# A layernorm's reciprocal deviation by Newton's steps on GpSimd, in a layernorm, attention and feed-forward kernel

## The chip, the cores and the metric

The kernel runs on one core of one Trainium2 chip. The metric is the device time of one execution in microseconds, as the median of several runs. Engines are named as the profile does: PE is TensorE, PEld its weight load, DVE is VectorE, ACT is ScalarE, POOL is GpSimd, SP is SyncE, which here only issues DMAs.

## The reference

Four sequences of 512 tokens and 512 features are normalized; the normalized tokens go through causal attention with 16 heads of 128 and, beside it, through a gated feed-forward network; the attention's output times silu of the network's is added to the input.

```python
def _layernorm(x, axis=-1, eps=1e-05):
    m = jnp.mean(x, axis=axis, keepdims=True)
    v = jnp.var(x, axis=axis, keepdims=True)
    return (x - m) / jnp.sqrt(v + eps)

x = L0_attn_x                              # (4, 512, 512)
xn = _layernorm(x, axis=-1)
s = _L0_attn_ref(xn, W_Q, W_K, W_V, W_O, b_Q, b_K, b_V, b_O)   # causal softmax attention
g = _silu(_L0_ffn_ref(xn, gate_w, up_w, down_w, gate_s, up_s, down_s))
x = x + s * g
```

Only the normalization changes. It is a small part of the work, but everything else of a batch starts from it.

## The kernel before

Tokens are worked in tiles of 128 on the partitions: a batch has four tiles (NT = 4), a row of features four chunks (ND = 4). Every operand of a matmul is kept as a high part and a low part (`Split`), and a product is made of three matmuls, so each result that TensorE leaves in PSUM is taken out twice: ScalarE writes the high part (L295, L321, L358, L516), then VectorE subtracts it from the PSUM value for the low part (L296, L323, L359, L517).

The order of work on each engine is the order of the program text (`manual_schedule`). Each engine works through its own queue in that order, and an instruction that waits holds up all behind it.

**Layernorm of a batch.** `ln_stats` makes mean and variance of each tile on VectorE (two instructions for each tile, L226 and L227). `ln_sd` takes the square root for all four tiles on ScalarE (L234), for which the activation table must be changed; `table` (L243) loads the exponential's table again with a dummy activation. `ln_scales` makes the reciprocal and the shift, minus mean times reciprocal, on VectorE (L255, L257), each 128x4. `ln_normalize` makes the normalized tile xn, on VectorE (L273) or, for some tiles, on ScalarE (L270). `ln_transposes` turns it on TensorE (L290) into a PSUM tile `tr`; ScalarE copies that to xh (L295) and VectorE subtracts to xl (L296, `ln_low`). Batch 0 is normalized tile by tile ahead of everything; batches 1, 2 and 3 are normalized among the attention heads.

**The loop over heads.** A step n is a head (g, b, i): head group g (eight, of two heads each), batch b, head i of the group. For group 0 these are heads 0 and 1 for batch 0, heads 2 and 3 for batch 1, and so on. In one step the program issues:

1. `softmax` of this head: score matmuls (L104, L394, L395) into PSUM tiles `sc`, masked maxima on VectorE (L403), exponentials on ScalarE (L417), reciprocals of the sums on VectorE (L420), and the scaling p times rtot on GpSimd (L423), each for row tiles of 512, 384, 256 and 128 columns. A list `between` is worked off between these.
2. `split_p` of the head before (for the first heads; later after step 3): probabilities that came back from DRAM transposed (`ptr`) are cast on ScalarE (L470) and subtracted on VectorE (L472, both inputs in SBUF; `pt`).
3. v projections of the first two tiles, then `turn_p`: VectorE transposes the scaled p in 32x32 blocks (L437) and a DMA writes them to DRAM and four DMAs read them back (`turn`, `ptr`).
4. `project`: q and k of the next head (L104, taken out in L358 and L359).
5. `attend` of the head before: z (L504, taken out in L516 and L517), then v projections of the other two tiles or the output projection (`pso`, L93 to L95, added up in L560 and L563).

Batch 1 is normalized in step 0, batch 2 in step 2, batch 3 in step 4 (`ln_next`); their statistics are made in steps 0 (and shortly ahead of it), 1 and 3. The transposes of the normalized tiles are mixed into the v projection's matmuls: a list `side` is popped once after each matmul, and begins with a few empty entries, so that the transposes start late enough. The v projection of a tile can also be begun early (`begin_v`, `finish_v`).

PSUM has eight banks: three for `st` (scores, and the `tr` tiles of batches 1 to 3 but the last of each) and five for `mm` (q, k, v, z, output projection, the last `tr`), taken in turn. A tile that has not been read out for its low part holds its bank, and TensorE waits for it. From group 1 on, `chores` do other work for the network on GpSimd (L608) and VectorE. The network follows the last head.

Of the kernel before, what the change touches and what calls it, by code (L numbers as in the profile page):

```python
# [10 lines left out]
F32 = mybir.dt.float32  # L11
# [7 lines left out]
P = 128  # L19
HG = 2  # L20
IGNORE = -100000.0
EPS = 1e-5
BIG = 3.0e38
WARM = 20
# [18 lines left out]
def kernel(  # L43
# [78 lines left out]
    with ExitStack() as at:  # L122
# [21 lines left out]

        here.tile([P, 8], F32, name="pad")
        ident = here.tile([P, P], F32, name="ident")
# [104 lines left out]
        def ln_scales(b):  # L251

            mv, sd = sd_of.pop(b)
            rstd = small.tile([P, NT], F32, name="rstd4", bufs=2)
            nc.vector.reciprocal(rstd, sd)  # L255
            add = small.tile([P, NT], F32, name="shift", bufs=2)
            nc.vector.scalar_tensor_tensor(add, mv[:, :, 0], -1.0, rstd, ALU.mult, ALU.mult)  # L257
            scaled[b] = rstd, add

        def ln_normalize(b, t, on_scalar=False):  # L260
            xt = x_in.pop((b, t))
            mv, sd = ln_of.pop((b, t))
            xn = lnp.tile([P, D], F32, name="xn")
            if b in scaled:
                rstd, add = (a[:, t : t + 1] for a in scaled[b])
            else:
                rstd = small.tile([P, 1], F32, name="rstd")
                nc.vector.reciprocal(rstd, sd)
            if on_scalar:
                nc.scalar.activation(xn, xt, AF.Identity, bias=add, scale=rstd)  # L270
                xn_of[b, t] = xn
                return
            nc.vector.tensor_scalar(xn, xt, mv[:, 0:1], rstd, ALU.subtract, ALU.mult)  # L273
            xn_of[b, t] = xn
# [101 lines left out]

        def softmax(qT, kT, between):
            p = pp.tile([P, NS * P], F32, name="p", tag="p")
# [34 lines left out]
            for pack in PACK:  # L413
                for t in pack:
                    tot = small.tile([P, 1], F32, name="tot", bufs=8)
                    rtot = small.tile([P, 1], F32, name="rtot", bufs=8)
                    nc.scalar.activation(  # L417
                        of[t], of[t], AF.Exp, bias=nmax[t], scale=-1.0, accum_out=tot
                    )
                    nc.vector.reciprocal(rtot, tot)  # L420
                    if len(between) > NT // 2:
                        between.pop(0)()
                    nc.gpsimd.tensor_scalar(of[t], of[t], rtot, 1.0, ALU.mult, ALU.mult)  # L423
# [213 lines left out]
        with tc.manual_schedule():  # L637
# [34 lines left out]
            for low, on in zip(wv_lows, (nc.gpsimd, nc.vector)):  # L672
                low(on)
            prepare_qk(1, -1)

            q_of = project(0, 0, wq[0], bq_sb, "q", 2, by_pass=True)
# [11 lines left out]
            ln_low(0, 2)  # L688
            ln_low(0, 3)
            table(AF.Exp)  # L690
            for _ in v_first:
                pass
            v_second = project_v_steps(0, 0, 1)
            next(v_second)
            for t in range(NT):
                load_x(1, t)
            for of in (q_of, k_of) * 3:
                next(of)
            qT = next(q_of)
            mv = ln_stats(1, range(NT), slice(0, 1))  # L700
            kT = next(k_of)
            split_pending(-1)
            ln_stats(1, range(NT), slice(1, 2), mv)
            for _ in v_second:
# [28 lines left out]
            for n, (g, b, i) in enumerate(heads):  # L733
# [26 lines left out]
                if ln_next:  # L760
                    norms = [lambda: ln_scales(b + 1)] + [
                        lambda t=t: ln_normalize(b + 1, t, t < NT // 2 if n > 0 else t == NT - 1)
                        for t in ((2, 3, 0, 1) if n > 0 else range(NT))
                    ]
                if ln_next and 0 not in begun and n > 0:

                    begin_v(g, b, 0)
                elif 0 in begun:
                    finish_v(0)
                of = softmax(qT, kT, norms if n > 0 else [])  # L770
                if n > 0 and early:
# [6 lines left out]
                if n == 0:  # L778
                    ln_stats(ln_b, range(NT), slice(2, NT), mv)
                if nxt is not None:  # L780
# [4 lines left out]
                if nxt is not None:  # L785
                    if ln_b is not None and n > 1:
                        ln_stats(ln_b, range(NT))
                    nh = nxt[0] * HG + nxt[2]
                    if n == 0:
                        ln_sd(ln_b, range(NT))  # L790
                        table(AF.Exp)
                        while norms:
                            norms.pop(0)()
                    *_, qT = project(nxt[1], nh, wq[nh], bq_sb, "q")
# [24 lines left out]
                if g > 0:  # L819
                    next(chore)  # L820
                if n == 2:

                    begin_v(g, b, half)
                if before is not None:
                    attend_last(before, pt)
                if n == 1:
                    ln_stats(ln_b, range(NT))
                if n == 1:

                    begin_v(nxt[0], nxt[1], 0)  # L830
                    next(begun[0])
                if ln_b is not None and n > 0:
                    ln_sd(ln_b, range(NT))
                    table(AF.Exp)
                if ln_next:
                    side.extend([lambda: None] * (2 * ND + (NT - 1 if n == 0 else 0)))
                    for t in range(NT):
# [589 lines left out]
```

## Time and profile before

| | us |
|---|---|
| median of 3 runs | 1196.64 (1196.04 to 1197.71) |
| the profiled execution, its own time | 1196.86 |
| its span, from the first to the last instruction | 1195.1 |

| engine | busy us | share of the span |
|---|---|---|
| PE | 1184.2 | 99% |
| DVE | 921.7 | 77% |
| ACT | 608.2 | 51% |
| POOL | 453.9 | 38% |

The granted TensorE clock is 0.999 of full speed over the span. A line of the timeline gives start, duration, engine, line, operation, output and inputs, shape, and how many instructions it merges; in brackets is the engine's idle time just before it and what ended it. A merged line has the shape of its first instruction. In the table of waits the numbers are total time, times and the longest. Matmuls are pipelined and their ends are modelled, so small gaps between them are best read from their starts.

### The profile page before, as it was taken

Reading aid. Unit: us, or ns where it says so; the run is one execution under the profiler, and the core shown is the slowest. Engines: PE = TensorE matmul, PEld = TensorE weight load, DVE = VectorE, ACT = ScalarE, POOL = GpSimd, SP = SyncE. Lnnn points to the kernel's source line nnn. Section 1 sums busy time; section 2 is a strip of 40 time slices with the busy share of each in tenths; the row PEclk is TensorE's granted clock in tenths of the full one; section 3 lists DMA queues with packets and bytes.
Section 4 is the critical chain, followed back from the end, with each engine's and each line's share of the span. In section 5 each row is a group of like instructions: output and inputs, shape, how many; then the busy total and the mean of one; then the engine's idle time right before and its main releaser. Section 6 shows DMA issues by size and latency. Waiting matters only on the chain.

```text
span 1195.1 us, 20226 instructions
## 1 busy us (share of the span) xinstructions
PE 1184.2 (99%) x6478; PEld 1036.2 (87%) x6478; DVE 921.7 (77%) x2485; ACT 608.2 (51%) x1455; POOL 453.9 (38%) x636
## 2 busy tenths in 40 slices
PE   9999999999999999999999999999999999999997
PEld 8888888888888888888888888888888888989896
DVE  7887777778777877787878777877777778959574
ACT  6764444545455545544554454545454454637372
POOL 4312342434253424342443344324232374636250
PEclk9999999999999999999999999999999999999999
DMA  5554456666675667566756676766565797969691
GB/s 167 156 181 152 148 165 208 203 194 211 194 218 179 203 202 223 172 214 205 225 183 205 199 229 175 216 185 197 164 183 156 215 328 233 265 203 267 179 264 56
DMA packets 131506, 236.75 MB, mean 198 GB/s; under 512 B 14912, under 2 KB 58688, under 8 KB 131392
## 3 DMA queue, kind: packets, MB, share of 16 engines
q1 hardware_dynamic: 73584, 133.86, 36.4%
q10 hardware_dynamic: 29520, 53.40, 15.4%
q0 software_dynamic: 28288, 48.12, 14.2%
q8 instruction: 54, 0.88, 0.3%
q14 instruction: 60, 0.49, 0.1%
HBM read 150.51 MB, written 84.80 MB: 197 GB/s over the span
## 4 chain that ended last, share of the span: by engine, by line
PE 98%; DVE 1%; DMA 0%; ACT 0%; issue 0%
PE psq L104 15%; PE psk L104 15%; PE psv L330 9%; PE z L504 9%; PE sc L104 8%; PE pd L1151 7%; PE px L981 6%; PE pso L93 5%; PE pso L94 5%; PE pso L95 5%; PE psv L334 4%; PE pz L981 3%; PE psv L104 2%; PE py L981 2%; PE pu L981 1%; PE pg L981 1%
## 5 line engine op out<-in xcount | busy, mean ns | idle before, releaser
L423 POOL TENSOR_SCALAR p<-p,rtot 128x512 f32<-128x512 f32 (+3 forms) x256 | 136.5, 554 | 434.2 <-DVE rtot L420 413.4
L417 ACT ACTIVATE p<-p,nmax 128x512 f32<-128x512 f32 (+3 forms) x256 | 140.9, 552 | 122.8 <-DVE nmax L403 122.7
L330 PE MATMUL psv<-wv,xh 128*128 128x512 f32 x448 | 124.6, 400 | 0.0
L437 DVE STREAM_TRANSPOSE sq<-p 128x256 f32<-128x256 f32 x378 | 113.3, 363 | 0.0
L104 PE MATMUL sc<-k,q 128*128 128x512 f32 (+2 forms) x576 | 112.1, 338 | 1.2 <-DVE xl L296 0.8
L104 PEld LDWEIGHTS sc<-k,q 128*128 128x128 f32 x576 | 98.9, 188 | 12.4 <-ACT xh L295 1.0
L358 ACT ACTIVATE k<-psk,consts 128x512 fp32r<-128x512 f32 (+1 forms) x65 | 44.4, 683 | 114.0 <-PE psk L104 114.0
L403 DVE CUSTOM_DVE_ANT_0 p<-sc,mask 128x512 f32<-128x512 f32 (+2 forms) x192 | 96.2, 550 | 0.6 <-PE sc L104 0.4
L470 ACT CAST pt<-ptr 128x640 fp32r<-128x640 f32 x126 | 85.2, 725 | 17.7 <-DMA ptr<-turn 10.7
L359 DVE SCALAR_TENSOR_TENSOR k<-psk,consts,k 128x512 fp32r<-128x512 f32 (+1 forms) x65 | 48.0, 739 | 58.5 <-ACT k L358 58.5
L472 POOL TENSOR_TENSOR pt<-ptr,pt 128x640 fp32r<-128x640 f32 x53 | 83.7, 1579 | 19.1 <-ACT pt L470 14.3
L330 PEld LDWEIGHTS psv<-wv,xh 128*128 128x128 f32 x448 | 76.0, 188 | 10.0
L334 PEld LDWEIGHTS psv<-wv,xl 128*128 128x128 f32 x448 | 68.4, 188 | 9.5
L420 DVE RECIPROCAL rtot<-tot 128x1 f32<-128x1 f32 x256 | 41.5, 162 | 41.2 <-ACT p L417 34.4
L563 DVE TENSOR_TENSOR a<-pso,a 128x512 f32<-128x512 f32 x108 | 69.6, 684 | 3.6 <-DMA a<-acc 3.2
L334 PE MATMUL psv<-wv,xl 128*128 128x256 f32 x448 | 71.0, 280 | 0.0
L1151 PE MATMUL pd<-wd,hl 128*128 128x512 f32 (+1 forms) x187 | 69.7, 378 | 0.0
L472 DVE TENSOR_TENSOR pt<-ptr,pt 128x640 fp32r<-128x640 f32 x73 | 67.8, 940 | 2.4 <-ACT pt L470 2.3
L1151 PE MATMUL pd<-wd,hh 128*128 128x512 f32 (+1 forms) x187 | 69.6, 377 | 0.0
L358 ACT ACTIVATE q<-psq,consts 128x512 fp32r<-128x512 f32 (+1 forms) x65 | 44.3, 681 | 42.1 <-PE psq L104 41.8
L970 POOL DMA_DIRECT2D ws<-sum x78 | 41.5, 540 | 37.5 <-PE px L981 34.3
L504 PE MATMUL z<-pt,v_0h 128*128 128x512 f32 x128 | 50.6, 396 | 0.1
(623 smaller groups left out, 3258.6 us busy)
## 6 DMA issues: line engine op xcount, KB each, us to landing
turn<-sq SPq DMA_DIRECT2D x63, 640.0 KB, 2.9
ptr<-turn SPq DMA_DIRECT2D x252, 160.0 KB, 5.4
acc<-a SPq DMA_DIRECT2D x124, 256.0 KB, 2.8
a<-acc ACTq DMA_DIRECT2D x108, 256.0 KB, 3.1
ws<-sum POOLq DMA_DIRECT2D x39, 384.0 KB, 4.8
wg<-in_gate_w POOLq DMA_DIRECT2D x44, 256.0 KB, 4.9
sum<-sums SPq DMA_DIRECT2D x22, 256.0 KB, 5.7
wu<-in_up_w POOLq DMA_DIRECT2D x44, 128.0 KB, 4.6
```

The source lines that it names most:

```text
L104: nc.tensor.matmul(ps, getattr(a, i), getattr(b, k), start=m + n == 0, stop=m == len(passes) - 1 and n == len(pairs) - 1,)
L330: nc.tensor.matmul(ps, x_[c].hi, wv[g].both[:, :, c, :], start=c == 0, stop=False)
L334: nc.tensor.matmul(ps[:, 1], x_[c].lo, wv[g].hi[:, c, :], start=False, stop=c == ND - 1)
L358: nc.scalar.activation(q.hi[:, at_], ps, AF.Identity, bias=bias[:, h : h + 1])
L403: nc.vector.tensor_tensor_reduce(out=of[t], in0=where[t], in1=add, scale=-SCALE, scalar=BIG, op0=ALU.add, op1=ALU.min, accum_out=nmax[t],)
L417: nc.scalar.activation(of[t], of[t], AF.Exp, bias=nmax[t], scale=-1.0, accum_out=tot)
L423: nc.gpsimd.tensor_scalar(of[t], of[t], rtot, 1.0, ALU.mult, ALU.mult)
L437: nc.vector.transpose(dst.rearrange("p a s i -> p s a i"), src.rearrange("p (s a i) -> p s a i", s=n, i=Q),)
L472: on.tensor_tensor(dst(pt.lo), src, dst(pt.hi32), ALU.subtract)
L504: nc.tensor.matmul(o, v, p_, start=k == 0, stop=k == len(todo) - 1)
L981: nc.tensor.matmul(ps, l, r, start=not more and k == 0, stop=k == len(todo) - 1, skip_group_check=more,)
L1151: nc.tensor.matmul(self.ps, part, wd[f][:, self.c], start=f == 0 and part is h_.hi, stop=f == NF - 1 and part is h_.lo,)
```

## The change

`ln_scales` computes the reciprocal deviation without a square root. From variance plus eps it makes a first guess by integer arithmetic on the number's bits, then takes three Newton steps, each y times (1.5 - 0.5 v y y), for all four tiles of a batch at once: 17 instructions on GpSimd, on 128x4. `ln_sd` and the table changes around it go for batches 1 to 3; batch 0 keeps the old way. The instructions land as follows.

- Batch 1: its tiles of x are loaded earlier in the program text (their place in SP's queue is the same); all four statistics are made ahead of step 0, among the first projections, and `ln_scales` is issued ahead of step 0 too, in front of the loads of `bo_bc` and `ds_bc` on GpSimd's queue. Two of the normalizations on VectorE go ahead of `turn_p`, one behind it.
- Batch 2: two statistics stay at the end of step 1, two move into step 2's softmax, after the first and the second reciprocal; `ln_scales` follows there, so on GpSimd it stands between the second and the third scaling of p. The normalizations on VectorE stand behind the pt subtractions and one v subtraction, ahead of the transposes of `turn_p`; before, they were among the reciprocals.
- Batch 3: the statistics stay, `ln_scales` stands at the end of step 3 where `ln_sd` was.
- In step 2 the v projection of tile 2 is no longer begun ahead of z; it comes whole after z, so more transposes are mixed with matmuls. In step 0 `side` begins with 8 empty entries instead of 11.
- An unused tile `pad` grows from 8 to 40 columns.

```diff
@@ -20,6 +20,7 @@
 HG = 2
 IGNORE = -100000.0
 EPS = 1e-5
+NEWTON = 3
 BIG = 3.0e38
 WARM = 20
 LOW_BITS = (1 << 12) - 1
@@ -142,7 +143,7 @@
             x_in[b, t] = xt
 
 
-        here.tile([P, 8], F32, name="pad")
+        here.tile([P, 40], F32, name="pad")
         ident = here.tile([P, P], F32, name="ident")
         mask = here.tile([P, S], F32, name="mask")
         eps = here.tile([P, 1], F32, name="eps")
@@ -250,20 +251,38 @@
 
         def ln_scales(b):
 
-            mv, sd = sd_of.pop(b)
+
+
+
+            mv = mv_of.pop((b, tuple(range(NT))))
             rstd = small.tile([P, NT], F32, name="rstd4", bufs=2)
-            nc.vector.reciprocal(rstd, sd)
             add = small.tile([P, NT], F32, name="shift", bufs=2)
-            nc.vector.scalar_tensor_tensor(add, mv[:, :, 0], -1.0, rstd, ALU.mult, ALU.mult)
-            scaled[b] = rstd, add
+            neg = small.tile([P, NT], F32, name="neg", bufs=2)
+            sq = small.tile([P, NT], F32, name="newton", bufs=2)
+            on = nc.gpsimd
+            on.tensor_scalar(sq, mv[:, :, 1], EPS, 1.0, ALU.add, ALU.mult)
+            on.tensor_scalar(neg, sq, -0.5, 1.0, ALU.mult, ALU.mult)
+            on.tensor_scalar(
+                rstd.bitcast(I32), sq.bitcast(I32), -0.5, float(0x5F3759DF), ALU.mult, ALU.add
+            )
+            for _ in range(NEWTON):
+                on.tensor_tensor(sq, rstd, rstd, ALU.mult)
+                on.tensor_tensor(sq, sq, neg, ALU.mult)
+                on.tensor_scalar(sq, sq, 1.5, 1.0, ALU.add, ALU.mult)
+                on.tensor_tensor(rstd, rstd, sq, ALU.mult)
+            on.tensor_scalar(add, mv[:, :, 0], -1.0, 1.0, ALU.mult, ALU.mult)
+            on.tensor_tensor(add, add, rstd, ALU.mult)
+            scaled[b] = mv, rstd, add
 
         def ln_normalize(b, t, on_scalar=False):
             xt = x_in.pop((b, t))
-            mv, sd = ln_of.pop((b, t))
             xn = lnp.tile([P, D], F32, name="xn")
             if b in scaled:
-                rstd, add = (a[:, t : t + 1] for a in scaled[b])
+                mv, *rest = scaled[b]
+                mv = mv[:, t, :]
+                rstd, add = (a[:, t : t + 1] for a in rest)
             else:
+                mv, sd = ln_of.pop((b, t))
                 rstd = small.tile([P, 1], F32, name="rstd")
                 nc.vector.reciprocal(rstd, sd)
             if on_scalar:
@@ -374,7 +393,7 @@
         row = [t * (t + 1) // 2 * P for t in range(NT)]
         slot = [j * NT - j * (j - 1) // 2 for j in range(NT)]
 
-        def softmax(qT, kT, between):
+        def softmax(qT, kT, between, keep):
             p = pp.tile([P, NS * P], F32, name="p", tag="p")
             of = [p[:, row[t] : row[t] + (t + 1) * P] for t in range(NT)]
             nmax = {}
@@ -418,7 +437,7 @@
                         of[t], of[t], AF.Exp, bias=nmax[t], scale=-1.0, accum_out=tot
                     )
                     nc.vector.reciprocal(rtot, tot)
-                    if len(between) > NT // 2:
+                    if len(between) > keep:
                         between.pop(0)()
                     nc.gpsimd.tensor_scalar(of[t], of[t], rtot, 1.0, ALU.mult, ALU.mult)
             return of
@@ -672,6 +691,8 @@
             for low, on in zip(wv_lows, (nc.gpsimd, nc.vector)):
                 low(on)
             prepare_qk(1, -1)
+            for t in range(NT):
+                load_x(1, t)
 
             q_of = project(0, 0, wq[0], bq_sb, "q", 2, by_pass=True)
             k_of = project(0, 0, wk[0], bk_sb, "k", 2, by_pass=True)
@@ -687,20 +708,20 @@
             ln_transpose(0, 3)
             ln_low(0, 2)
             ln_low(0, 3)
+            mv = ln_stats(1, range(NT), slice(0, 1))
             table(AF.Exp)
             for _ in v_first:
                 pass
+            ln_stats(1, range(NT), slice(1, 2), mv)
             v_second = project_v_steps(0, 0, 1)
             next(v_second)
-            for t in range(NT):
-                load_x(1, t)
             for of in (q_of, k_of) * 3:
                 next(of)
             qT = next(q_of)
-            mv = ln_stats(1, range(NT), slice(0, 1))
             kT = next(k_of)
             split_pending(-1)
-            ln_stats(1, range(NT), slice(1, 2), mv)
+            ln_stats(1, range(NT), slice(2, NT), mv)
+            ln_scales(1)
             for _ in v_second:
                 pass
             bo_bc = load_const(here, b_o.broadcast_to([P, D]), [P, D], "bo_bc")
@@ -758,16 +779,23 @@
 
                 norms = []
                 if ln_next:
-                    norms = [lambda: ln_scales(b + 1)] + [
+                    norms = [
                         lambda t=t: ln_normalize(b + 1, t, t < NT // 2 if n > 0 else t == NT - 1)
                         for t in ((2, 3, 0, 1) if n > 0 else range(NT))
                     ]
+                if n == 2:
+
+                    rest = [
+                        lambda t=t: ln_stats(b + 1, range(NT), slice(t, t + 1), mv)
+                        for t in (2, 3)
+                    ]
+                    norms = rest + [lambda: ln_scales(b + 1)] + norms
                 if ln_next and 0 not in begun and n > 0:
 
                     begin_v(g, b, 0)
                 elif 0 in begun:
                     finish_v(0)
-                of = softmax(qT, kT, norms if n > 0 else [])
+                of = softmax(qT, kT, norms if n > 0 else [], NT if n == 2 else NT // 2)
                 if n > 0 and early:
                     pt = split_p(raw, B * HG < n < len(heads) - 2)
                 half = NT // 2 if nxt is not None else NT - 1
@@ -776,7 +804,8 @@
                     while norms:
                         norms.pop(0)()
                 if n == 0:
-                    ln_stats(ln_b, range(NT), slice(2, NT), mv)
+                    while len(norms) > NT // 2:
+                        norms.pop(0)()
                 if nxt is not None:
                     raw_next = turn_p(of)
                 if not early:
@@ -786,11 +815,8 @@
                     if ln_b is not None and n > 1:
                         ln_stats(ln_b, range(NT))
                     nh = nxt[0] * HG + nxt[2]
-                    if n == 0:
-                        ln_sd(ln_b, range(NT))
-                        table(AF.Exp)
-                        while norms:
-                            norms.pop(0)()
+                    while norms:
+                        norms.pop(0)()
                     *_, qT = project(nxt[1], nh, wq[nh], bq_sb, "q")
                 if nxt is not None:
                     *_, kT = project(nxt[1], nh, wk[nh], bk_sb, "k")
@@ -818,22 +844,18 @@
                         prepare_qk((g + 1) * HG + 1, (g + 1) * per_g)
                 if g > 0:
                     next(chore)
-                if n == 2:
-
-                    begin_v(g, b, half)
                 if before is not None:
                     attend_last(before, pt)
                 if n == 1:
-                    ln_stats(ln_b, range(NT))
+                    mv = ln_stats(ln_b, range(NT), slice(0, 2))
                 if n == 1:
 
                     begin_v(nxt[0], nxt[1], 0)
                     next(begun[0])
-                if ln_b is not None and n > 0:
-                    ln_sd(ln_b, range(NT))
-                    table(AF.Exp)
+                if ln_b is not None and n > 1:
+                    ln_scales(ln_b)
                 if ln_next:
-                    side.extend([lambda: None] * (2 * ND + (NT - 1 if n == 0 else 0)))
+                    side.extend([lambda: None] * (2 * ND))
                     for t in range(NT):
                         side.extend(ln_transposes(b + 1, t))
                         side.append(lambda t=t: ln_low(b + 1, t))
```

## Prediction

> **What bounds the kernel now.** I read the page's busy times first, then TensorE's waits, then the timeline head by head from 8 to 90 us, where the batches are normalized.
>
> ```profile
> PE 1184.2 (99%) x6478; PEld 1036.2 (87%) x6478; DVE 921.7 (77%) x2485; ACT 608.2 (51%) x1455; POOL 453.9 (38%) x636
> ```
>
> TensorE has 10.9 us of idle time in 1195.1, and most lies at the start (2.5 us before 10 us) and in the feed-forward part (7.1 us after 950 us), which the change leaves alone. TensorE's own waits (us in total, times, longest) hold little for it:
>
> ```profile
> PE psq L104 <- DVE xh L293: 0.9, 1, 0.9
> PE sc L104 <- DVE xl L296: 0.8, 1, 0.8
> PE sc L104 <- DVE k L359: 0.4, 1, 0.4
> ```
>
> Measured from matmul start to matmul start against the usual pitch, the stretch loses 0.6 us at 18.4 (the low part of k stands behind a statistic on VectorE), 0.3 at 32 and 1.0 at 57 (both wait for an xl subtraction to give its PSUM buffer back). So at most 2.0 us can be gained. No table load stands among these waits. But VectorE is over 80% busy from 20 to 80 us, so little is needed to make it late. These lines of the timeline (start, duration) are the places where the new work lands: first head 0 on GpSimd, then head 2, then what TensorE waits for.
>
> ```profile
> 20.94 0.72 POOL L152 DMA_DIRECT2D bo_bc<-in_b_o  x1
> ...
> 21.66 0.55 POOL L152 DMA_DIRECT2D ds_bc<-in_down_s  x1
> ...
> 22.39 2.06 POOL L423 TENSOR_SCALAR p<-p,rtot 128x512 f32<-128x512 f32 x4 [0.17 <-DVE rtot L420]
> ```
>
> ```profile
> 48.13 3.61 POOL L423 TENSOR_SCALAR p<-p,rtot 128x512 f32<-128x512 f32 x4 [7.35 <-DVE rstd L255]
> ...
> 49.96 1.62 DVE L472 TENSOR_TENSOR pt<-ptr,pt 128x640 fp32r<-128x640 f32 x2
> ...
> 51.84 1.79 DVE L437 STREAM_TRANSPOSE sq<-p 128x256 f32<-128x256 f32 x6
> ```
>
> ```profile
> 57.21 2.47 DVE L296 TENSOR_TENSOR xl<-tr,xh 128x512 fp32r<-128x512 f32 x4
> 58.04 1.82 PE L104 MATMUL sc<-k,q 128*128 128x512 f32 x9 [0.79 <-DVE xl L296]
> ...
> 63.20 1.36 ACT L470 CAST pt<-ptr 128x640 fp32r<-128x640 f32 x2 [0.52 <-DMA ptr<-turn]
> ```
>
> **What is removed.** ScalarE loses six table loads of 1.28 us, three square roots of 0.30 and three dummies of 0.20: 9.2 us, none on TensorE's path. VectorE loses three small reciprocals and three shifts, about 1 us. The moved statistics cost the same 0.8 us each.
>
> **The price of one Newton chain.** It is 17 GpSimd instructions on 128x4, a form the trace lacks. The undisturbed L423 scalings last 0.69, 0.58, 0.47 and 0.36 us for 512 to 128 columns, so 0.26 at four. Two-input subtractions last 1.29 (512) and 0.735 (256), so 0.20 at four. What a dependent instruction adds is seen in the chores:
>
> ```profile
> 155.70 0.75 POOL L608 TENSOR_TENSOR sums<-looku 128x256 f32<-128x256 f32 x1
> 156.53 1.20 POOL L608 TENSOR_TENSOR sums<-sums,lookg 128x256 f32<-128x256 f32 x1
> 157.69 0.74 POOL L608 TENSOR_TENSOR sums<-lookg,looku 128x256 f32<-128x256 f32 x1
> ```
>
> The second needs the first and starts 0.08 us after its end; the third does not need the second and starts 0.04 before its end. Fourteen of the 17 are dependent. Opening: 0.26 + 0.34 + 0.22 = 0.82. Each step: three two-input ones at 0.28 and one at 0.34 = 1.18, three steps 3.54; rstd stands after 4.4 us. The shift adds 0.22 + 0.28: 4.9 us. From below, all at the 0.10 us of a 128x1 memset: 14 x 0.18 + 3 x 0.06 = 2.7. From above, all at the 0.38 of a 128x128 scaling: 14 x 0.46 + 3 x 0.34 = 7.5. I take 4.9, since it extends the same kinds of instruction.
>
> A rule that speaks against the change: the Trainium skill, "GPSIMD Engine Reference", section 4.1, gives elementwise work to VectorE and calls GpSimd about twice as slow for two inputs. Twice VectorE's 0.16 us for the 128x4 shift would make 17 x 0.32 = 5.4 us, an estimate, and the sum below 1 us larger.
>
> **Head 0 (batch 1).** The statistics move ahead of q, so k's low part runs at 17.9 instead of 18.67 and TensorE gains its 0.6 us. GpSimd is free at 20.95 (before, the two DMA issues stood here). Newton runs to 25.85, the issues, which now stand behind it, to 27.1, and only then come the softmax scalings: 4.7 us later than 22.39, to 29.2. On VectorE the six transposes wait for these and end at 29.5 instead of 26.67. The third normalization is queued behind them (to 30.0), so are the low parts of q and k, and the xl. TensorE wants the third tile's transposes at 28.7 and gets them at 30.1. q starts at 30.0 instead of 28.39, so every xl is 1.6 us later, less the 0.33 of a v subtraction now behind the third: the last score pack, before at 32.31, starts at 33.6. TensorE: +1.3. Softmax of head 1: +1.6.
>
> **Head 1.** The turn through DRAM started 2.9 us later; its last load, issued at 34.6, lands by 37.9 at the usual 3.3 us, and the pt casts go from 35.75 to 37.9. TensorE's own lateness of 1.3 covers that: z is wanted at 39.8 (pt high part at 39.2), k's low part at 43.6 (there at 43.3). VectorE is 1.9 late at z0l, saves two statistics (1.6), and begins head 2's softmax at 45.8 (45.52 before). ScalarE's table load, which held the exponentials until 47.04, is gone, and this alone would bring them to 46.6; the statistics eat it.
>
> **Head 2 (batch 2).** VectorE does its maxima, rtot, then statistic, rtot, statistic: done at 49.6. Newton starts there, between the second and third scalings. The two pt subtractions run at the same time (49.6 to 51.2). Before, the last scaling met them too: the four at 48.13 took 3.61 instead of 2.06 us, the last 1.58 instead of 0.37, held out until both were over. So Newton does its second instruction after 51.2; rstd at 55.5, the end at 55.9. Queued behind on GpSimd: the last two scalings, to 56.9. On VectorE the two normalizations that wait for rstd stand ahead of the transposes, and they ahead of q and k. Transposes end at 58.5 instead of 53.57: +4.9. On ScalarE the other two normalizations wait, tile 0 done at 56.8. TensorE, 1.3 late, wants it after z and nine v matmuls at 54.6: a stall of 2.2. The v projection that stood ahead of z covers it no more; z itself finds pt's high part ready, so that move costs nothing by itself. Then q, k, z1l, v and xl follow from 58.5: xl are done at 61.5, 62.1 and 62.7 and each frees a score buffer; the output projection starts at 63.4 instead of 59.87. TensorE: +3.55.
>
> The trace's 1.58 against "SBUF — State Buffer", section "Who interferes with whom": there, an instruction holds the shared ports for itself alone and issue order decides. By that, Newton could enter between the two subtractions, 0.8 us earlier, and the sum would be 0.8 smaller.
>
> **Head 3.** The turn is 4.9 late, so are the casts, subtractions, transposes and the four statistics behind them. q's low part goes from 71.53 to 76.5.
>
> ```profile
> 71.53 0.72 DVE L359 SCALAR_TENSOR_TENSOR q<-psq,consts,q 128x512 fp32r<-128x512 f32 x1
> ...
> 72.81 0.64 PE L104 MATMUL psv<-wv,xh 128*128 128x256 f32 x4
> ```
>
> That v matmul takes q's PSUM buffer (five in the ring). It would be due at 76.4 and starts at 77.2: +0.85, in all +4.4. The third Newton chain (76.5 to 81.4) is hidden: GpSimd's next scaling, before at 77.37, is then due at 82. The enlarged pad only moves addresses: nothing.
>
> **The sum.** Span 1195.1 + 4.4 = 1199.5; the profiled execution took 1196.86, 0.2 over the median of 1196.64, so 1201.0 for the median. Newton's time counts at head 0 and again at head 2, nearly 2 us for each us of it. Worked the same way, 2.7 us makes about +0.2: the gains at 18, 32 and 57 are used up by q's buffer in head 3. 7.5 makes about +9.4.
>
> **The rivals.** (1) Cheap instructions: GpSimd's cost on four columns is the memset's. For it: that row; against it: a memset reads nothing. 1196.8. (2) Faster: the chains hide wholly, the three stalls go and nothing replaces them: 1194.6. For it: GpSimd is 38% busy. It decides only from about 1.7 us a chain, 0.1 us an instruction with its wait, and the measured 0.08 of waiting leaves 0.02. (3) Dear instructions: 0.38 each, or more where VectorE shuts GpSimd out: 1206.0. (4) It does not do what it says: the order of instructions of the changed program has none of the six loads left, so no chance.
>
> **Numbers.** Forecast 0.55, cheap 0.23, hidden 0.06, dear 0.16. The 80% range leaves out the hidden case and the far end of the dear one: 1195.8 to 1205.0. About 0.2% (2.4 us) is what a measurement can tell from no change. Slower by more, over 1199.0, is the forecast but for chains under some 3.9 us, and the dear case: 0.72. Even the hidden case gains only 0.17%, so faster gets 0.04; the rest, 0.24, is the same.
>
> **Right or wrong.** Right: GpSimd's L423 of head 0 starts near 27, its 128x4 rows take 0.2 to 0.3 us at a pitch of about 0.29, and TensorE waits over 2 us for a normalized tile near 55. Wrong: a chain under 3 us, scores of head 1 at or before 30.8, or no wait of TensorE for xn in head 2.

## The result and the profile after

| | before | after |
|---|---|---|
| median, us | 1196.38 (6 runs) | 1201.61 (6 runs, 1200.96 to 1202.59) |
| ratio of the times | | 1.0043, 95% interval 1.003 to 1.0056 |
| the profiled execution, us | 1196.86 | 1201.91 |
| its span, us | 1195.1 | 1200.1 |

The kernel became slower by 5.2 us (3.6 to 6.7 by the interval). The first line of the page after:

```profile
PE 1183.5 (99%) x6478; PEld 1035.2 (86%) x6478; DVE 917.4 (76%) x2479; ACT 598.6 (50%) x1443; POOL 461.9 (38%) x687
```

ScalarE gave up 9.6 us of work and VectorE 4.3; GpSimd took on 8.0. TensorE does the same work in the same time, so the 5 us are waits of its own. TensorE's waits after (total us, times, longest):

```profile
PE tr L309 <- DVE xn L292: 2.3, 2, 1.5
PE tr L309 <- ACT xn L289: 1.6, 1, 1.6
...
PE z L523 <- ACT pt L489: 1.4, 1, 1.4
PE psv L105 <- DVE q L378: 1.2, 1, 1.2
```

Before, xn stood there with 0.2 us, and pt and q not at all. (Of the 2.3 us for xn on VectorE, 0.8 lie at the start, where batch 0 is normalized, before 12 us.) The timeline says where each belongs. GpSimd's queue at head 0: the chain (its first and last instruction and two in the middle), the two DMA issues behind it, and only then the scalings, which stood at 22.39 before.

```profile
20.69 0.19 POOL L263 TENSOR_SCALAR newton<-mv 128x4 f32<-128x4 f32 x1
...
21.50 0.20 POOL L269 TENSOR_TENSOR newton<-rstd 128x4 f32<-128x4 f32 x1
21.78 0.20 POOL L270 TENSOR_TENSOR newton<-newton,neg 128x4 f32<-128x4 f32 x1
...
25.02 0.40 POOL L274 TENSOR_TENSOR shift<-shift,rstd 128x4 f32<-128x4 f32 x1
25.36 0.76 POOL L153 DMA_DIRECT2D bo_bc<-in_b_o  x1
26.13 0.55 POOL L153 DMA_DIRECT2D ds_bc<-in_down_s  x1
26.71 2.07 POOL L442 TENSOR_SCALAR p<-p,rtot 128x512 f32<-128x512 f32 x4
```

The same queue at head 2. Two instructions here last 0.88 and 0.64 us instead of 0.20; they run while VectorE makes its two pt subtractions (the next fence). The scalings, split in two by the chain, go on at 57.15.

```profile
51.31 0.19 POOL L263 TENSOR_SCALAR newton<-mv 128x4 f32<-128x4 f32 x1 [0.21 <-DVE rtot L439]
...
52.40 0.88 POOL L270 TENSOR_TENSOR newton<-newton,neg 128x4 f32<-128x4 f32 x1
53.37 0.64 POOL L271 TENSOR_SCALAR newton<-newton 128x4 f32<-128x4 f32 x1
...
57.15 1.12 POOL L442 TENSOR_SCALAR p<-p,rtot 128x256 f32<-128x256 f32 x2
```

VectorE at head 2: ahead of the two normalizations it stands idle for 2.26 us until rstd is there, and the transposes of p behind them end at 59.29 instead of 53.63.

```profile
52.40 1.56 DVE L491 TENSOR_TENSOR pt<-ptr,pt 128x640 fp32r<-128x640 f32 x2 [1.08 <-ACT pt L489]
53.88 0.41 DVE L342 TENSOR_TENSOR v_1l<-psv,v_1h 128x256 fp32r<-128x256 f32 x1
56.56 1.00 DVE L292 TENSOR_SCALAR xn<-xt,mv,rstd 128x512 f32<-128x512 f32 x2 [2.26 <-POOL rstd L272]
57.48 1.81 DVE L456 STREAM_TRANSPOSE sq<-p 128x256 f32<-128x256 f32 x6
```

The four waits of TensorE that carry the loss, in order of time (the number in brackets is the idle time just before the line's first matmul):

```profile
29.84 0.30 PE L309 MATMUL tr<-ident,xn 128*128 128x128 f32 x1 [1.48 <-DVE xn L292]
...
41.01 0.50 PE L523 MATMUL z<-pt,v_0h 128*128 128x512 f32 x1 [1.41 <-ACT pt L489]
...
58.06 0.33 PE L309 MATMUL tr<-ident,xn 128*128 128x128 f32 x1 [1.57 <-ACT xn L289]
...
78.54 0.74 PE L105 MATMUL psv<-wv,xh 128*128 128x256 f32 x4 [1.16 <-DVE q L378]
```

Counted from matmul start to matmul start against the usual pitch, TensorE lost 1.64 at 28 us, 0.72 at 31, 1.57 at 39, 1.73 at 56, 0.77 at 62 and 1.32 at 77: 7.75 us between 16 and 120 us, where the kernel before lost 1.68. The difference of 6.07 is more than the 4.97 that the span grew. Part of the rest is a start: the first score matmul stood 0.44 us earlier in this execution (0.04 to 0.54 earlier in those of the experiments, whatever they changed). The rest is given back after 500 us: 0.29 at about 530 us, most of what remains behind the last head's scores.

How late the first score matmul of each head is against before shows where the time was lost, beside what the prediction said of it:

| stretch | start before | start after | lost in the stretch, us | predicted, us |
|---|---|---|---|---|
| up to head 0's scores | 18.18 | 17.74 | -0.44 | 0 |
| head 0, up to head 1's | 30.78 | 32.09 | +1.75 | +1.3 |
| head 1, up to head 2's | 41.85 | 44.47 | +1.31 | 0 |
| head 2, up to head 3's | 58.04 | 62.47 | +1.81 | +2.25 |
| head 3, up to head 4's | 74.25 | 80.07 | +1.39 | +0.85 |
| head 4 to the end | 1195.1 (end) | 1200.1 (end) | -0.85 | 0 |
| span | 1195.1 | 1200.1 | +4.97 | +4.4 |

### The profile page after: what moved, and what is told of

Its sections match the earlier page's. It is cut to its first block, busy times and chain, and to the rows that moved or that the text cites. A ratio compares the mean times of both kernels' runs of the same rounds, so it can differ in the third digit from the quotient of the medians.

```text
span 1200.1 us, 20260 instructions
## 1 busy us (share of the span) xinstructions
PE 1183.5 (99%) x6478; PEld 1035.2 (86%) x6478; DVE 917.4 (76%) x2479; ACT 598.6 (50%) x1443; POOL 461.9 (38%) x687
## 4 chain that ended last, share of the span: by engine, by line
PE 93%; DVE 2%; DMA 2%; POOL 1%; issue 1%; ACT 1%; SPq 0%; ACTq 0%; POOLq 0%
PE psq L105 13%; PE psk L105 13%; PE psv L349 9%; PE z L523 8%; PE sc L105 8%; PE pd L1173 7%; PE px L1003 6%; PE pso L94 5%; PE pso L95 5%; PE pso L96 5%; PE psv L353 4%; PE pz L1003 3%; PE py L1003 2%; PE psv L105 1%; DMA ptr<-turn 1%
## 5 line engine op out<-in xcount | busy, mean ns | idle before, releaser
L442 POOL TENSOR_SCALAR p<-p,rtot 128x512 f32<-128x512 f32 (+3 forms) x256 | 133.5, 540 | 415.6 <-DVE rtot L439 415.5
L491 DVE TENSOR_TENSOR pt<-ptr,pt 128x640 fp32r<-128x640 f32 x73 | 64.3, 892 | 7.2 <-ACT pt L489 7.2
```

The costliest lines, as they stand in the source:

```text
L491: on.tensor_tensor(dst(pt.lo), src, dst(pt.hi32), ALU.subtract)
```

## The experiments

The theory: the chain's own length delays what stands behind it, the scalings of head 0 and the normalizations and scalings of head 2, and TensorE waits for it in both heads. Its rivals: the loss comes from the moved statistics and the other order on VectorE, not from the chain; the third chain, behind head 3, costs time too; and, of the wait for pt at head 1 that had not been foreseen, that it comes from the loads of `bo_bc` and `ds_bc`, which now meet the turn through DRAM. Each expectation tells its theories with their numbers.

All kernels are the changed one with switches: `MODE` picks, for each batch, the new text or that of before at every place that the diff touches, `NEWTON` is the number of steps, `LATE_BO` moves the loads of `bo_bc` and `ds_bc`. Line numbers are up to 12 higher for that. The edits below are shown as the switches resolve them; the modes `early` and `start` are told where they come in. Each was timed beside the kernel before on the same chip (its median there is 1196.1 to 1196.8).

### No steps (e1), and five (e2)

```diff
-NEWTON = 3
+NEWTON = 0    # and 5
```

> The changed kernel with all three Newton steps left out, so the deviation is only the first guess: five GpSimd instructions for a batch in place of 17, everything moved stays moved. In the changed kernel's trace a step's instruction takes 0.277 us from start to start, so the chain falls from 4.7 to about 1.4 us. Theory A (the chain's time is paid at head 0 and again at head 2, near 2 us for each us, until the waits that the kernel before had are used up): 1194.7 to 1197.0, no wait of TensorE over 1 us for a normalized tile. Rival B (the loss comes from where statistics, normalizations and the v projection were moved, not from the chain): 1200 to 1202 as before. Rival C (the loss is the DRAM round trip of the probabilities meeting the other loads): about 1199 to 1200, with the wait of z for pt left over.

Measured: 1196.9 us against 1196.75, ratio 1.0002 (0.9993 to 1.0012), as theory A expected. GpSimd's five remaining instructions take 1.3 us at head 0 (21.01 to 22.30). Between 16 and 120 us TensorE's waits come to 1.99 us by starts, against 1.68 before. The longest is at z of head 1; none is for xn:

```profile
PE z L535 <- ACT pt L501: 1.1, 1, 1.1
```

> The changed kernel with five Newton steps: eight instructions more, 2.2 us for each chain. Theory A: 2.2 times nearly 2, so 1201.6 + 4.3 = 1205.9 (1204 to 1207.5). Rival B: 1201.6 to 1202.5. Rival C: 1203 to 1204, since only the round trip of head 0 is pushed out further.

Measured: 1207.4 us against 1196.75, ratio 1.0092 (1.0076 to 1.0109), within theory A's range, at its upper end. The chain of head 0 runs from 21.08 to 28.0, 2.2 us longer than with three steps, and the waits for normalized tiles grow to

```profile
PE tr L321 <- ACT xn L301: 3.7, 1, 3.7
PE tr L321 <- DVE xn L304: 3.5, 2, 2.1
```

With the statistics moved, the order changed and only the steps gone, no loss is left, so the rival of the moved statistics falls; the time follows the length of the chain. From 1.3 to 4.7 us a chain the median rises by some 4.7 us, from 4.7 to 6.9 by 5.8, so by 2.6 us for each us once the slack is used up. (That figure is a quotient of two differences, and the interval of e2 alone is 4 us wide.)

### One batch at a time (e3, e4, e5)

```diff
+MODE = {1: "new", 2: "old", 3: "old"}   # batch 1 alone
+MODE = {1: "old", 2: "new", 3: "old"}   # batch 2 alone
+MODE = {1: "old", 2: "old", 3: "new"}   # batch 3 alone
```

> Only batch 1 in the new way (statistics ahead, Newton in front of head 0's scalings); batches 2 and 3 as in the kernel before, with their square roots and table loads. Theory A: head 0's part alone, +1.3 us on the scores of head 1 and up to 1.6 at z for the late pt: 1198.5 to 1200. Rival B (the statistics and normalizations inside head 2 are what costs): 1195.5 to 1196.5, with the gain of 0.6 us at the first scores kept.

Measured: 1200.51 us against 1196.75, ratio 1.0033 (1.002 to 1.0046); above the expected 1198.5 to 1200. TensorE waits for the third normalized tile (1.63 us by starts), at head 1's scores (0.73), and 1.03 us for pt at z of head 1.

> Only batch 2 in the new way (two statistics and Newton inside head 2's softmax, no early v projection); batches 1 and 3 as before. Theory A: VectorE starts head 2 some 1.6 us earlier than in the changed kernel did, the chain ends near 53.6 instead of 57, the turn of head 2 is some 2.4 us later than before, and the sum is 1197.5 to 1199.5. Rival B: nearly the whole loss, 1200 to 1202.

Measured: 1198.01 us against 1196.75, ratio 1.001 (1.0 to 1.0019), within theory A's range, and hardly clear of no change. The wait for the first normalized tile of head 2 is 0.84 us by starts, half of that after:

```profile
PE tr L321 <- ACT xn L301: 0.7, 1, 0.7
PE sc L107 <- ACT v_3h L352: 0.6, 1, 0.6
```

> Only batch 3 in the new way: its Newton chain stands at the end of head 3, where GpSimd is idle; batches 1 and 2 as before. Theory A: the chain is covered, 1196.3 to 1197.0, no new wait of TensorE. Rival D (each chain costs about the same wherever it stands): a third of the loss, 1198.4.

Measured: 1196.28 us against 1196.11, ratio 0.9999 (0.999 to 1.0009), with the three waits of before unchanged. The third chain costs nothing that can be measured: it lies in a stretch where GpSimd waits anyway. Batch 1 alone costs 3.8 us, batch 2 alone 1.3, batch 3 nothing: about 5.1 together, near the 5.2 of the whole. Each of these has an interval of 1 us or more to either side, so that the parts add up is not proved by it, and the wait for xn at head 2 is not the same alone (0.84 us) as with batch 1 changed too (1.73).

### The two DMA issues behind the chain (e6, e9)

```diff
-            bo_bc = load_const(here, b_o.broadcast_to([P, D]), [P, D], "bo_bc")
-            ds_bc = load_const(const, down_s.broadcast_to([P, D]), [P, D], "ds_bc")
...
                 of = softmax(qT, kT, ...)
+                if n == 0:         # e6; in e9: n == 1
+                    bo_bc, ds_bc = load_bc()
```

> The changed kernel with the two DMA issues (bo_bc, ds_bc) moved on GpSimd's queue from behind the first Newton chain to behind head 0's four scalings. That takes 1.3 us out of the way of the scalings, the chain itself is untouched. Theory A (what counts is the time at which the scalings come): scalings at 25.4 instead of 26.7, TensorE's wait for the third tile falls from 1.6 to about 0.4, that of z from 1.6 to 0.3: 1199.0 to 1200.2. Theory C (the wait of z comes from loads that meet on the DMA engines): these loads now meet the turn and the read back even more, z's wait stays, 1200.4 to 1201.6.

Measured: 1201.27 us against 1196.11, ratio 1.004 (1.0025 to 1.0056). The 1199.0 to 1200.2 that earlier scalings alone would give was missed; the 1200.4 to 1201.6 of the collision held. The scalings do start 1.28 us earlier (25.43) and the wait for the third tile falls from 1.64 to 0.63 us. But the turn gives most of it back: it is issued 1.0 us earlier than after, and its casts start only 0.4 us earlier. SyncE's queue in e6 (the write, then the read back, which waits for the write):

```profile
28.28 0.33 SPq L473 DMA_DIRECT2D turn<-sq  x1
32.82 1.81 SPq L479 DMA_DIRECT2D ptr<-turn  x4
```

And the casts on ScalarE that wait for the read:

```profile
39.18 1.35 ACT L501 CAST pt<-ptr 128x640 fp32r<-128x640 f32 x2 [3.09 <-DMA ptr<-turn]
```

The write takes 4.5 us, with two loads of 256 KB now beside the whole of it, against 3.6 after, and TensorE waits 2.13 us for pt.

> The changed kernel with the two DMA issues moved further, behind head 1's scalings, where no probabilities are on their way through DRAM. In the run with the issues behind head 0's scalings the scalings came 1.3 us earlier and TensorE waited 1.0 us less for the third tile, but z waited 0.8 us more, since the two loads now met the turn's write (landing 4.5 us after its issue instead of 3.6). Theory A with C as its second part (head 0's loss goes through two gates: the scalings for the transposes, the round trip for z): scalings at 25.4, write landing 3 us after its issue, z's wait gone or under 0.4: 1198.0 to 1199.6. If the loads do not matter and z's wait has another cause: 1200.6 to 1201.6.

Measured: 1198.69 us against 1196.54, ratio 1.0023 (1.0014 to 1.0033), as expected. The same two views of e9:

```profile
28.18 0.33 SPq L473 DMA_DIRECT2D turn<-sq  x1
31.17 1.76 SPq L479 DMA_DIRECT2D ptr<-turn  x4
```

```profile
36.61 1.36 ACT L501 CAST pt<-ptr 128x640 fp32r<-128x640 f32 x2 [0.65 <-DMA ptr<-turn]
```

The write takes 2.9 us, the casts start 3.0 us earlier than after (39.60), and the wait for pt is gone. Moving two DMA issues, with all three chains left in, takes back about half of the loss. Not all of that follows from the two loads: of the 3.0 us, 1.1 is the earlier issue of the write and 0.6 its shorter time, but 1.25 is the latest of the four reads, which landed after 4.0 us here and after 5.3 in the changed kernel, and on that see the section on the landing below.

### The second chain out of head 2 (e7, e10)

```diff
+MODE = {1: "old", 2: "early", 3: "new"}     # e7; in e10 batch 1 is "new"
...
                 if n == 1:
-                    mv = ln_stats(ln_b, range(NT), slice(0, 2))
+                    ln_stats(ln_b, range(NT))
...
-                if ln_b is not None and n > 1:
+                if ln_b is not None and n > 0:
                     ln_scales(ln_b)
```

The normalizations on VectorE stand among head 2's reciprocals again, as before the change. In e7 the v projection of tile 2 is begun ahead of z again, too; in e10 it stays behind.

> Batches 1 as before; batch 2's four statistics stay together at the end of head 1 as before, and its Newton chain (three steps) stands there too, where GpSimd has nothing to do for some 3 us before head 2's scalings; the normalizations stand where they stood before; batch 3 new. ScalarE has no table load between the heads 1 and 4. Theory A: the chain ends near 50, delays the first scalings by some 1.7 us but not the last, which waits for the pt subtractions anyhow: 1195.8 to 1197.2. Rival D: 1198 to 1200.

Measured: 1196.33 us against 1196.11, ratio 1.0001 (0.9992 to 1.001), as theory A expected. The chain runs at 45.02 to 49.77. The first reciprocal of head 2's softmax is there at 47.27, so the chain does hold up the scalings (49.75 instead of 48.13 before), and they end at 53.31 instead of 51.74:

```profile
49.75 3.56 POOL L454 TENSOR_SCALAR p<-p,rtot 128x512 f32<-128x512 f32 x4
50.28 1.85 DVE L503 TENSOR_TENSOR pt<-ptr,pt 128x640 fp32r<-128x640 f32 x2
...
52.39 1.79 DVE L468 STREAM_TRANSPOSE sq<-p 128x256 f32<-128x256 f32 x6
```

VectorE is busy with the pt subtractions meanwhile, the transposes of p start 0.55 us later than before (51.84), and TensorE's waits are those of before (0.54, 0.20, 0.96 by starts). All statistics on VectorE ahead of the softmax cost nothing that is measured.

> The changed kernel, but batch 2's four statistics and its chain of three steps stand at the end of head 1, ahead of head 2's scalings on GpSimd, and its normalizations among the reciprocals as in the kernel before; the v projection stays behind z as in the change. Head 0 is as in the change. Theory A: head 0's part, 3.8 us as measured with batch 1 alone, stays, head 2's part goes: 1199.4 to 1200.6, with no wait over 0.5 us of TensorE for a normalized tile at head 2. If the two parts are not separate, below 1199 or still 1201.6.

Measured: 1199.85 us against 1196.54, ratio 1.0028 (1.0017 to 1.0039), within theory A's range. The wait for xn at head 2 is gone, but z of head 2 now waits 1.26 us by starts for pt, which was not foreseen. VectorE's queue shows why:

```profile
52.99 0.55 DVE L304 TENSOR_SCALAR xn<-xt,mv,rstd 128x512 f32<-128x512 f32 x1 [1.87 <-POOL rstd L284]
...
54.10 1.85 DVE L503 TENSOR_TENSOR pt<-ptr,pt 128x640 fp32r<-128x640 f32 x2
```

The normalizations stand ahead of the pt subtractions in this order, so VectorE's wait for the chain (1.87 us) now delays pt, which TensorE wants first. In e7 VectorE waits as long (1.90 us), but there the chain starts at 45.02 and not, as here, at 48.86, and pt is still in time. So the wait of 1.73 us for xn did not go with the chain's new place; most of it moved to pt. What e10 gains over the changed kernel lies at the scores and the v matmul of head 3, whose waits (0.77 and 1.32 us after) are gone.

### A version that might beat both (e8, e11, e12)

```diff
-NEWTON = 3
+NEWTON = 2
+MODE = {1: "start", 2: "early", 3: "new"}
...
             for _ in v_second:
                 pass
+            ln_sd(1, range(NT))       # batch 1: root on ScalarE,
+            table(AF.Exp)             # the first exponential's table only after it
```

In e11 the v projection of head 2 stands whole behind z; in e12 the two DMA issues are moved behind head 1's scalings as well.

> A version meant to beat both: batch 1's four statistics are made ahead of head 0 as in the change, but its square root is taken on ScalarE while the root's table is still loaded from batch 0, so the load of the exponential's table only moves behind it; batches 2 and 3 take two Newton steps on GpSimd right behind their statistics, at the end of heads 1 and 3; normalizations as before. Theory A: the waits of the kernel before at 18, 32 and 57 us shrink and no new one comes: 1194.5 to 1196.0. If moving the statistics ahead is itself harmful (rival B): above 1197.

Measured: 1196.73 us against 1196.11, ratio 1.0003 (0.9994 to 1.0012): missed. Up to 120 us only 0.94 us of waits is left, and the heads run 1.2 us ahead of before, but at 261 and 290 us z waits 0.26 and 0.39 us for pt, and the span ends 0.13 under that of before.

> The version meant to beat both, with one more part of the change kept: batch 1's root on ScalarE before the exponential's table is first loaded, batches 2 and 3 with two Newton steps at the ends of heads 1 and 3, and the v projection of head 2 behind z, mixed with the transposes, as in the change. With the deviation cut to its first guess that mixing left 0.22 us of wait at the scores of head 3, where the kernel before and the earlier version have 0.94. So 0.7 us less than the earlier version up to head 3; in all 1194.8 to 1196.4, if the later waits of z for pt at heads 18, 20 and 52 come no oftener.

Measured: 1196.69 us against 1196.54, ratio 1.0003 (0.9994 to 1.0012): missed. The wait at 56 us is gone and z of head 1 waits 1.13 us for pt instead.

> The version with all that helped: batch 1's root on ScalarE before the first exponential, two Newton steps for batches 2 and 3 at the ends of heads 1 and 3, head 2's whole v projection behind z, and the loads of bo_bc and ds_bc issued behind head 1's scalings instead of ahead of head 0's. Theory A (waits alone count): the wait for pt at z of head 1, 1.1 us in the same version with the loads ahead of head 0's scalings, goes, since nothing shares the DMA engines with the turn's write; waits of 0.3 to 0.6 us are left up to 120 us, and the median comes out 0.8 to 1.2 us under that version's, 1195.4 to 1196.0 beside a kernel before of 1196.5, at most 0.1% faster. Theory B (given back later): heads from the eighth on wait for pt, and the median stays within 0.4 us of the kernel before, 1196.1 to 1196.9.

Measured: 1196.35 us against 1196.49, ratio 0.9999 (0.999 to 1.0008). The waits up to 120 us went, but for the one that the move of the loads was made for: z of head 1 still waits 0.97 us. The median lies where B put it, and z waited later in this execution too (0.53 us at 758). None of the versions beats the kernel before by an amount that can be measured.

### What the landing of the read back does

The wait for pt at head 1 came in some kernels and not in others, and the turn's write does not explain it alone. The trace has the time from issue to landing of the four reads. It also has loads of the program's instructions, 16 KB in one packet, which the page after lists among its DMA queues (packets, MB, share):

```profile
q8 instruction: 54, 0.88, 0.3%
```

One such load, lasting 0.9 to 1.7 us, falls near head 1's reads in every trace. The last column says when it begins, counted from the issue of the last read:

| kernel | write, us | latest read, us | instruction load begins, us |
|---|---|---|---|
| before, e4, e5, e7 (batch 1 as before) | 3.5 to 3.6 | 3.5 to 3.8 | 4.9 to 5.0 |
| after, e2, e3, e10 (DMA issues behind the chain) | 3.3 to 3.6 | 4.8 to 5.4 | 1.3 to 1.6 |
| e6 | 4.5 | 4.9 | 0.4 |
| e9 | 2.9 | 4.0 | 2.7 |
| e1 | 3.9 | 5.0 | 1.9 |
| e8 / e11 / e12 | 3.2 / 3.3 / 3.3 | 3.7 / 5.0 / 4.9 | 3.1 / 1.9 / 2.3 |

Wherever the instruction load begins within 2.3 us of the last read's issue, the latest read takes 4.8 us or more; at 2.7 it takes 4.0, and from 3.1 on 3.8 or less. The reads of the next turn, which meet no such load, take 3.5 to 3.7 us at the latest in all fourteen traces. e8 and e11 have the same instructions up to head 2 and fall on both sides, and so does their instruction load; e12 has no `bo_bc` load near the reads and a late read all the same. The loads of x issued right behind on the same queue are there in every kernel, late or not. So the trace points to the instruction load, and not to the loads of `bo_bc` and `ds_bc`, for the late read. No run moved it by itself: that it is the cause, and what sets its time, is not shown by experiment.

## Why the prediction came out as it did

The forecast held in total: 1201.0 against 1201.61. The mechanism that it named is there, the chain's length paid at head 0 and again at head 2, and none of its rivals came. Its parts held less well, and that the total is so close is in part luck.

**The price of the chain: 4.9, measured 4.7.** The kinds were off: one-input instructions take 0.19 us, not 0.26, as much as two-input ones (0.19 to 0.20), so the extrapolation from the scalings' widths failed there. The wait of 0.08 us was right: a dependent instruction starts 0.277 us after the one before it began. By the rule in the Trainium skill, "GPSIMD Engine Reference", section 4.1 (GpSimd about twice as slow as VectorE for two inputs) the estimate was 5.4, 0.7 more than measured; it took the factor for the one-input instructions too, which the section does not. At this width the rows don't show the factor: 0.20 us for two inputs on GpSimd, beside 0.16 to 0.18 for VectorE's shift. The cheap rival's 2.7 us was refuted by these rows, the dear one's 7.5 by the same.

**Head 0.** Scalings at 27.1 predicted, 26.71 measured; TensorE gets the third tile at 29.84 (30.1 predicted). The step held: head 1's scores start 1.31 us later than before, where 1.3 was predicted, although this execution was 0.44 us ahead when head 0 began, which makes the 1.75 us of the table.

**Head 1: the step that failed.** "the pt casts go from 35.75 to 37.9. TensorE's own lateness of 1.3 covers that". The casts came at 39.60. The turn's write was issued at 29.29 and read back at 32.92, close to what was assumed; the term that was mis-sized is the landing of the reads, taken at "the usual 3.3 us" from the last issue (the slowest at this place before took 3.8), when the slowest now took 5.3. With that z waits 1.57 us, head 2 begins 1.6 us later on VectorE (maxima at 47.43, predicted 45.8). A usual landing was taken where the latest of four decides, and nothing was set aside for its spread, nor for the instruction load that fell into it here. In e9, where the scalings come 1.3 us earlier and this wait is gone, the same three chains cost only 2.2 us.

**Head 2.** The chain starts at 51.31 (49.6 predicted), late by that same 1.6 to 1.7. The pt subtractions met it only at its fifth instruction, where the prediction had the second. They held up the two instructions of the fence by 0.69 and 0.45 us, 1.1 in all, where the prediction took 1.5 from the one scaling of before; between the two subtractions one instruction got through. That fits the Trainium skill, "SBUF — State Buffer", section "Who interferes with whom", which calls the ports that VectorE and GpSimd share an exclusive lock and says that issue order decides who blocks. It does not refute the row of before: other scalings were held through both subtractions too (1.60 us instead of 0.38 at head 1 of the kernel before, 1.81 instead of 0.59 at head 2 in e7), and what decides between the two outcomes is not shown. The stretch lost 1.81 us instead of 2.25: TensorE came later to the wait for xn. The 2.2 us of waiting became 1.73, so the sign of being right that asked for over 2 us there was missed.

**Head 3 and the third chain.** q's low part held the PSUM buffer as predicted, at 77.76 instead of 76.5, for 1.32 us instead of 0.85. The third chain is hidden, as e5 shows.

**No gain below.** The prediction said that a cheaper chain would only come back to the time before, and the hidden case would gain 0.17% at most. e1 (1.0002), e8, e11 and e12 fit this: the three stalls of before, 1.68 us, shrink or go in these versions, other waits come in their place (for pt, at z), and the measured time hardly moves; no version lost all of its waits, so what that would gain is not shown. And "nearly 2 us for each us" of chain was the right kind of number, somewhat low: 2.6 between three and five steps.

**Luck.** The errors nearly cancelled: 1.3 us more at head 1, 0.4 less at head 2, 0.5 more at head 3, 0.85 given back later, on which the prediction had nothing. One of its sums was off as well: "slower by more" at 0.72 is above the 0.55 and 0.16 that it was to be made of, which give 0.71 at most; and it took 53.57 for the end of the transposes before, where the line gives 51.84 + 1.79 = 53.63.

## What to carry to other kernels

Price a chain of tiny instructions by its dependent steps, not by its work, and then list everything that is queued behind it on that engine, DMA issues too: here 17 instructions of 0.2 us, with two DMA issues and a round trip through DRAM behind them, cost 3.8 us at one place and nothing that could be measured at two others (e5, e7), where the queue had time to spare. Busy time saved on an engine off the path (9.6 us of ScalarE) was worth nothing that could be measured here. Where several transfers must all have landed, reckon with the latest of them and with what else uses the DMA engines at that time, instruction loads too, and not with the median.

## What was not expected of the hardware

- GpSimd's instructions on 128x4 take 0.19 to 0.20 us with one input or two, also on int32, at 0.277 us from start to start when each needs the one before (the last of a chain with three steps is recorded with 0.40).
- One GpSimd instruction got in between two back-to-back VectorE subtractions with both inputs in SBUF; the two that met them lasted 0.88 and 0.64 us. Elsewhere a scaling was held through both (1.58 to 1.81 us).
- The turn's write of 640 KB landed after 2.9 us nearly alone (e9), 3.2 to 3.9 beside part of other loads, and 4.5 (e6) with two loads of 256 KB beside the whole of it.
- The slowest of four reads of 160 KB took 3.5 to 4.0 us in some executions, 4.8 to 5.4 in others, among them two kernels that are the same up to there. In all fourteen traces the late ones are those with a 16 KB instruction load beginning 0.4 to 2.3 us after the last read's issue.
